# Vector instructions that stay off the port shared with GpSimd: odd row counts for the normalization, a division in PSUM, and a band mask added in PSUM

## The chip, the cores and the metric

The kernel runs on one core of a Trainium2 chip. A core has a matrix engine (TensorE, PE in the profile; its weight loads are PEld), VectorE (DVE), ScalarE (ACT), GpSimd (POOL) and SyncE (SP), which here only starts transfers. SBUF is the working memory, PSUM the memory into which TensorE writes its products, in eight banks of 128 x 512 float32. The metric is the time of one execution on the device, in microseconds (us); the median of repeated runs counts.

## The reference

One layer over x of shape (2, 256, 128, 128): batch, time, band, channel, all float32. Three parts follow each other, each with a residual: attention over time with a causal mask, attention over the bands with a band mask of width 16, and a feed-forward part with gelu.

```python
xt = _ln(x, ln_t_w, ln_t_b).transpose(0, 2, 1, 3)
x = x + _mha(xt, t_wi, t_bi, t_wo, t_bo, 4, causal).transpose(0, 2, 1, 3)
xf = _ln(x, ln_f_w, ln_f_b)
x = x + _mha(xf, f_wi, f_bi, f_wo, f_bo, 4, band)      # band: |i - j| <= 16
xn = _ln(x, ln_n_w, ln_n_b)
h = gelu(xn @ w1.T + b1)
x = x + (h @ w2.T + b2)
```

## The kernel before

The tokens are worked on in groups of 512 (four tiles of 128). There are 128 groups of each part: `OverTime`, `OverBands` and `FeedForward`. All of `OverTime` comes first, then `OverBands` and `FeedForward` in turns of eight groups. Each pass of the loop in `run` works on several groups at once, each at another stage; the engines take their instructions in the order in which the program issues them. The names below (xh, z, sp, op, rp, yp, ...) are those of the profile.

The layer norm: statistics on VectorE, the root on GpSimd (as a power of -1/2), the normalization on VectorE, one instruction for each tile of 128 elements.

```python
def root(self):
    ...
    gpsimd.tensor_scalar(self.rstd, self.mv[:, :, 1], EPS, None, ALU.add)
    gpsimd.tensor_tensor(self.rstd, self.rstd, path.k.mhalf, ALU.pow)

def normalize(self):
    path, vector = self.path, self.path.vector
    self.xh = path.work.tile([P, NT, P], F32, name="xh", bufs=2)
    for i in range(NT):
        vector.tensor_scalar(
            self.xh[:, i, :], self.src()[:, i, :], self.mv[:, i, 0:1], self.rstd[:, i : i + 1],
            ALU.subtract, ALU.mult,
        )
```

`turn` transposes xh in blocks into z and sends it through DRAM (turned); `fetch` brings it back as xnT, the input of the products.

The softmax has no maximum: exponentials of the scores sp on ScalarE, masks on GpSimd, sums of the weights as a product with ones (rp), weighted values (op). The reciprocal of rp is exp(-ln(rp)) on ScalarE (r0, r in the profile), sharpened by one Newton step on VectorE, with op multiplied in. The sign is turned back by wn, which is -wo.

```python
def divide(self):
    ...   # the exact form, for 16 of 256 groups, is cut here
    t = path.work.tile([P, NT * P], F32, name="t", bufs=2)
    vector.tensor_tensor(by_rows(t), by_tile(self.rp), by_tile(self.r0), ALU.mult)
    u = path.work.tile([P, NT * P], F32, name="u", bufs=2)
    vector.tensor_tensor(by_rows(u), by_tile(self.op), by_tile(self.r0), ALU.mult)
    self.oT = path.work.tile([P, NT * P], F32, name="oT", bufs=2)
    vector.scalar_tensor_tensor(self.oT, t, 2.0, u, ALU.subtract, ALU.mult)

def output(self):
    self.yp = path.bank([P, NT, P], "yp")       # yp = oT times wn, by tiles
    ...
def finish(self):
    self.path.vector.tensor_tensor(self.dst(), self.yp, self.dst(), ALU.add)
```

In `OverTime` a group has two halves of scores, and GpSimd masks each after its exponentials. One sum of two blocks of weights (pt) for each half is done on GpSimd (`first_mask`) and on VectorE (`last_sum`). The residual with its row is added on GpSimd (`bias`): res<-x,orow in `OverTime`, x<-x,orow in `OverBands`, res<-x,rows_sb in `FeedForward`.

In `OverBands` GpSimd masks three heads with two selections each; the fourth is multiplied by a band of ones and zeros on VectorE.

```python
def first_function(self):
    for h in range(H):
        self.path.scalar.activation(self.p[:, h].rearrange("p i q -> p (i q)"), self.sp[h], AF.Exp)

def second_mask(self):
    path = self.path
    for h in range(H - self.by_vector, H):       # by_vector = 1
        blk = self.p[:, h]
        path.vector.tensor_tensor(blk, blk, path.band.unsqueeze(1).to_broadcast([P, NT, P]), ALU.mult)
```

All PSUM tiles come from one pool of eight banks. The order of a pass:

```python
do(n + 11, "load")
do_at(n + 4, OverTime, "statistics")
...
do_at(n + 4, FeedForward, "root")
do(n, "first_half", "first_function", "first_mask")
...
do_at(n + 2, FeedForward, "normalize", "turn")
do_at(n + 3, Attention, "normalize", "turn")
do_at(n + 4, OverTime, "root")
if bands[2]:
    do(n, "second_mask")
do(n - 1, "weigh")
do(n - 1, "invert_exactly" if turn else "invert")
if bands[2] or turn:
    do(n - 2, "output", "finish")
do(n - 1, "divide")
do_at(n + 5, FeedForward, "statistics")
...
do(n + 1, "queries_keys", "take_query", "take_key")
if not bands[2] and not turn:
    do(n - 2, "output", "finish")
do(n + 1, "values", "take_values")
do(n, "last_sum")
```

Of the kernel before, what the change touches and what calls it, by code (L numbers as in the profile page):

```python
# [10 lines left out]
F32 = mybir.dt.float32  # L11
BF16 = mybir.dt.bfloat16
I32 = mybir.dt.int32
AF = mybir.ActivationFunctionType
# [5 lines left out]
P = 128  # L20
H = 4
# [404 lines left out]
def by_rows(t):  # L426

    return t.rearrange("p (t i q) -> p i t q", i=NT, q=D)


def by_tile(t):

    return t.rearrange("p (i t q) -> p i t q", i=NT, q=D)


class Group:
# [31 lines left out]
        gpsimd.tensor_tensor(self.rstd, self.rstd, path.k.mhalf, ALU.pow)  # L468

    def normalize(self):  # L470
        path, vector = self.path, self.path.vector
        self.xh = path.work.tile([P, NT, P], F32, name="xh", bufs=2)
        for i in range(NT):
            vector.tensor_scalar(
                self.xh[:, i, :], self.src()[:, i, :], self.mv[:, i, 0:1], self.rstd[:, i : i + 1],
                ALU.subtract, ALU.mult,
            )

    def turn(self):
# [19 lines left out]
    def first_function(self):  # L499
        pass  # L500
# [10 lines left out]
    def second_mask(self):  # L511
        pass
# [35 lines left out]
class Attention(Group):  # L548
# [51 lines left out]
    def divide(self):  # L600

        path, vector = self.path, self.path.vector
        if self.r0 is None:
            self.oT = path.work.tile([P, NT * P], F32, name="oT", bufs=2)
            u = path.work.tile([P, NT * P], F32, name="u", bufs=2)
            vector.tensor_tensor(by_rows(u), by_tile(self.op), by_tile(self.r), ALU.mult)
            vector.tensor_scalar(self.oT, u, -1.0, None, ALU.mult)
            return
        t = path.work.tile([P, NT * P], F32, name="t", bufs=2)
        vector.tensor_tensor(by_rows(t), by_tile(self.rp), by_tile(self.r0), ALU.mult)  # L610
        u = path.work.tile([P, NT * P], F32, name="u", bufs=2)
        vector.tensor_tensor(by_rows(u), by_tile(self.op), by_tile(self.r0), ALU.mult)
        self.oT = path.work.tile([P, NT * P], F32, name="oT", bufs=2)
        vector.scalar_tensor_tensor(self.oT, t, 2.0, u, ALU.subtract, ALU.mult)

    def output(self):
        path = self.path
# [114 lines left out]
class OverBands(Attention):  # L732
# [12 lines left out]
                path.tensor.matmul(self.sp[h][:, c], self.kT[r, c], self.qT[r, c], start=True, stop=True)  # L745

    def first_function(self):
        for h in range(H):
            self.path.scalar.activation(self.p[:, h].rearrange("p i q -> p (i q)"), self.sp[h], AF.Exp)

    def first_mask(self):
        path = self.path
        for h in range(H - self.by_vector):
            blk = self.p[:, h]
            for s in (1, -1):
# [1 line left out]
                    out=blk, in_=blk, compare_op=ALU.is_ge, fill=path.zero, base=BAND,  # L757
                    pattern=[[0, NT], [-s, P]], channel_multiplier=s,
                )

    def second_mask(self):
        path = self.path
        for h in range(H - self.by_vector, H):
            blk = self.p[:, h]
            path.vector.tensor_tensor(blk, blk, path.band.unsqueeze(1).to_broadcast([P, NT, P]), ALU.mult)

    def first_half(self):
        self.p = self.path.work.tile([P, H, NT, P], F32, name="pf", tag="p", bufs=2)
# [84 lines left out]
class BoundedPath:  # L853
    def __init__(self, ctx, tc, k):
        self.tc, self.nc, self.k = tc, tc.nc, k
        self.xpool = ctx.enter_context(tc.tile_pool(name="xpool", bufs=3))
        self.work = ctx.enter_context(tc.tile_pool(name="work", bufs=3))
        self.small = ctx.enter_context(tc.tile_pool(name="small", bufs=6))
        self.ps = ctx.enter_context(tc.tile_pool(name="ps", bufs=8, space=PSUM))
        self.tensor, self.vector = InOrder(tc, tc.nc.tensor), InOrder(tc, tc.nc.vector)  # L860
        self.scalar, self.gpsimd = InOrder(tc, tc.nc.scalar), InOrder(tc, tc.nc.gpsimd)
        self.dram = ctx.enter_context(tc.tile_pool(name="turns", bufs=3, space=DRAM))
        self.zero = 0.0
        once = ctx.enter_context(tc.tile_pool(name="once", bufs=1))

        self.band = once.tile([P, P], F32, name="band")
        tc.nc.gpsimd.memset(self.band, 1.0)
        for s in (1, -1):
            tc.nc.gpsimd.affine_select(
                out=self.band, in_=self.band, compare_op=ALU.is_ge, fill=0.0, base=BAND,  # L870
                pattern=[[-s, P]], channel_multiplier=s,
            )

# [14 lines left out]
    def quad(self, held, name, bufs):  # L888

        held[name] = self.xpool.tile([P, NT, NT, P], F32, name=name, tag=name, bufs=bufs)  # L890

    def groups(self, x, out):
        nc, k = self.nc, self.k
# [2 lines left out]
        for b in range(B):  # L896
            for f0 in range(0, FB, GA):
# [14 lines left out]
                            self.of_times(k.x1[b], i, slice(f - 1, f + 1)), held["res"][rows_of(i), :, g - 1 : g + 1]  # L912
                        )

                def part(name, g, held=held):
                    if name == "res" and name not in held:
                        self.quad(held, "res", 2)
                    return held[name][:, :, g]

                for g in range(NT):  # L920
                    yield OverTime(self, partial(part, "x", g), partial(part, "res", g), partial(load, g), partial(store, g))
        for b in range(B):
            for r0 in range(0, T, RUN):
                run = []
                for t0 in range(r0, r0 + RUN, GB):
# [17 lines left out]
                                held["res"][rows_of(i), g - 1 : g + 1].rearrange("q g t c -> q (g t) c"),  # L943
                            )

                    def part(name, g, held=held):
                        if name == "res" and name not in held:
                            self.quad(held, "res", 2)
                        return held[name][:, g]

                    run += [(g, part, load, store) for g in range(NT)]
# [5 lines left out]
    def run(self, x, out):  # L957
        groups = list(self.groups(x, out))

        def do(n, *names):  # L960
            if 0 <= n < len(groups):
                for name in names:
                    getattr(groups[n], name)()
# [11 lines left out]
        for n in range(-11, len(groups) + 2):  # L975
# [14 lines left out]
            do_at(n + 2, FeedForward, "normalize", "turn")  # L990
            do_at(n + 3, Attention, "normalize", "turn")
            do_at(n + 4, OverTime, "root")
            if bands[2]:
                do(n, "second_mask")
            do(n - 1, "weigh")
            do(n - 1, "invert_exactly" if turn else "invert")
            if bands[2] or turn:
                do(n - 2, "output", "finish")
            do(n - 1, "divide")
            do_at(n + 5, FeedForward, "statistics")  # L1000
            if not turn:
                do(n, "second_half", "second_function")
            if not bands[2]:
# [80 lines left out]
```

## Time and profile before

| what | value |
| --- | --- |
| time, median of 3 runs | 2785.62 us (2785.54 to 2787.24) |
| TensorE busy | 2730.3 us, 98% |
| VectorE busy | 2221.5 us, 80% |
| GpSimd busy | 2079.3 us, 75% |
| ScalarE busy | 1800.0 us, 65% |
| xh on VectorE | 1536 instructions, 392 ns each |
| t, u, oT on VectorE | 240 each, 667, 675 and 839 ns |
| the multiplication by the band (pf) on VectorE | 128 instructions, 935 ns each |
| res<-x,orow on GpSimd | 128 instructions, 1698 ns each |
| res<-x,rows_sb on GpSimd | 128 instructions, 1273 ns each |
| the power (rstd) on GpSimd | 384 instructions, 1149 ns each |

A line of the groups gives the source line, engine, operation, output<-inputs with shapes, the count, the busy time and the mean of one, and the idle time before them with what ended it. A line of the waits reads: engine and tile, what it waited for, then us in total, how often, and the longest. A line of the timeline gives start, duration, engine and operation; equal instructions in a row are merged, and an instruction's duration overlaps a little with the start of the next. Every operation goes through one helper, so all bear the line L848, and tiles tell them apart.

### The profile page before, as it was taken

The numbers are of one execution on the slowest core, as the hardware profiler recorded it, in microseconds if no ns is written. First come the engines' busy times: TensorE is split into PE (matmuls) and PEld (weight loads), VectorE is DVE, ScalarE is ACT, GpSimd is POOL, SyncE is SP. The second block draws the span as 40 slices with busy tenths as digits, with TensorE's granted clock in tenths as the row PEclk, the third lists the DMA queues.
The fourth block names the chain that finished last, engine by engine and source line by source line (L and its number), as shares of the span: only waits on it lengthen the run. The fifth ranks groups of instructions, "written<-read, shape, count | busy, mean of one in ns | idle before, by whom it ended". The sixth has DMA issues, their size and how long they took to land.

```text
span 2785.2 us, 103938 instructions
## 1 busy us (share of the span) xinstructions
PE 2730.3 (98%) x42534; PEld 1867.5 (67%) x42534; DVE 2221.5 (80%) x6446; ACT 1800.0 (65%) x3328; POOL 2079.3 (75%) x2569
## 2 busy tenths in 40 slices
PE   4999999999999989999999999999999999999998
PEld 3666666666666657776777777777777767767776
DVE  5888888888888898778678687687786786876874
ACT  2888888878888866646556556456466465574563
POOL 3899999999999997667676676676676666766762
PEclk9999999999999999999999999999999999999999
DMA  5555555555555554544544544535545445444333
GB/s 121 135 147 137 137 141 143 146 132 146 139 142 135 146 134 117 129 117 102 140 105 111 132 106 123 130 100 127 127 99 137 104 108 130 113 117 114 91 92 85
DMA packets 471301, 343.70 MB, mean 123 GB/s; under 512 B 43296, under 2 KB 405152, under 8 KB 470816
## 3 DMA queue, kind: packets, MB, share of 16 engines
q1 hardware_dynamic: 469568, 335.92, 47.5%
q8 instruction: 337, 5.52, 0.9%
q14 instruction: 148, 1.21, 0.2%
q10 hardware_dynamic: 1248, 1.05, 0.1%
HBM read 169.03 MB, written 167.77 MB: 121 GB/s over the span
## 4 chain that ended last, share of the span: by engine, by line
PE 93%; DVE 3%; DMA 2%; POOL 1%; issue 0%; SPq 0%; ACT 0%; DVEq 0%; POOLq 0%
PE zp L848 17%; PE hp L848 16%; PE sp L848 12%; PE op L848 10%; PE qp L848 8%; PE rp L848 8%; PE vp L848 8%; PE yp L848 7%; PE kp L848 7%; POOL pt L848 1%; DMA x<-in_x 1%; DVE xh L848 1%; DMA xnT<-turned 1%; DVE oT L848 0%; POOL rstd L848 0%; DVE stats L848 0%
## 5 line engine op out<-in xcount | busy, mean ns | idle before, releaser
L848 ACT ACTIVATE hT<-hp,b 128x512 f32<-128x512 f32 x512 | 348.7, 687 | 546.0 <-PE hp L848 536.1
L848 POOL TENSOR_SCALAR_AFFINE_SELECT pf<-pf 128x512 f32<-128x512 f32 x768 | 541.5, 720 | 173.5 <-ACT pf L848 147.1
L848 PEld LDWEIGHTS zp<-w2T_sb,hT 128*128 128x128 f32 x4096 | 476.4, 192 | 56.1 <-issue 54.0
L848 DVE TENSOR_SCALAR xh<-x,mv,rstd 128x128 f32<-128x128 f32 x1536 | 509.2, 392 | 0.4 <-POOL rstd L848 0.4
L848 PE MATMUL zp<-w2T_sb,hT 128*128 128x128 f32 x4096 | 479.8, 275 | 0.1
L848 PE MATMUL hp<-xnT,w1f 128*128 128x512 f32 x1024 | 469.2, 596 | 3.6 <-DMA xnT<-turned 3.4
L848 POOL TENSOR_TENSOR rstd<-rstd,mhalf 128x4 f32<-128x4 f32 x384 | 441.3, 1149 | 32.0
L848 ACT ACTIVATE pt<-sp 128x384 f32<-128x384 f32 x1024 | 419.5, 497 | 58.8 <-PE sp L848 58.8
L848 PE MATMUL sp<-qT,kT 32*128 32x128 f32 (+1 forms) x8192 | 389.5, 315 | 0.8 <-ACT kT L848 0.8
L848 POOL TENSOR_SCALAR_AFFINE_SELECT pt<-pt 128x512 f32<-128x512 f32 x512 | 322.7, 651 | 79.0 <-ACT pt L848 79.0
L848 PEld LDWEIGHTS sp<-qT,kT 32*128 32x128 f32 x8192 | 310.9, 185 | 79.7 <-issue 31.1
L848 POOL TENSOR_SCALAR rstd<-mv 128x4 f32<-128x4 f32 x384 | 89.2, 232 | 365.5 <-DVE mv L848 365.1
L848 DVE BATCH_NORM_STATS2 stats<-x 128x6 f32<-128x128 f32 x1536 | 329.0, 274 | 7.6 <-DMA x<-in_x 7.6
L848 ACT ACTIVATE pf<-sp 128x512 f32<-128x512 f32 x512 | 264.3, 603 | 58.8 <-PE sp L848 52.4
L848 PEld LDWEIGHTS hp<-xnT,w1f 128*128 128x128 f32 x1024 | 182.2, 190 | 178.9 <-issue 109.6
L848 PE MATMUL qp<-xnT,wf 128*32 128x512 f32 (+1 forms) x1856 | 273.1, 600 | 26.2 <-DVE xh L848 26.2
L848 PEld LDWEIGHTS yp<-wn,oT 128*32 128x32 f32 (+1 forms) x7808 | 240.8, 111 | 84.0 <-issue 63.2
L848 PEld LDWEIGHTS vp<-wf,xnT 128*32 128x32 f32 (+1 forms) x7424 | 241.1, 113 | 70.4 <-issue 60.2
L848 DVE STREAM_TRANSPOSE z<-xh 128x512 f32<-128x512 f32 x384 | 273.2, 711 | 18.9 <-DMA turned<-z 5.8
L848 PE MATMUL yp<-wn,oT 128*32 128x128 f32 (+1 forms) x7808 | 277.9, 273 | 0.3 <-DVE t L848 0.3
L848 DVE TENSOR_TENSOR res<-zp,res 128x512 f32<-128x512 f32 x128 | 87.6, 685 | 234.8 <-PE zp L848 234.7
L848 PE MATMUL vp<-wf,xnT 128*32 128x128 f32 (+1 forms) x7424 | 273.5, 273 | 0.5 <-DVE t L848 0.5
(90 smaller groups left out, 4072.8 us busy)
## 6 DMA issues: line engine op xcount, KB each, us to landing
turned<-z SPq DMA_DIRECT2D x1536, 64.0 KB, 2.2
xnT<-turned SPq DMA_DIRECT2D x384, 256.0 KB, 2.8
x<-in_x SPq DMA_DIRECT2D x128, 256.0 KB, 4.8
x<-res SPq DMA_DIRECT2D x256, 128.0 KB, 3.4
x<-x SPq DMA_DIRECT2D x128, 256.0 KB, 4.1
out<-res SPq DMA_DIRECT2D x256, 128.0 KB, 2.4
w1T_sb<-in_w1T ACTq DMA_DIRECT2D x1, 256.0 KB, 3.9
w2T_sb<-in_w2T ACTq DMA_DIRECT2D x1, 256.0 KB, 4.2
```

Of the source, the lines that this page charges most:

```text
L848: return self.tc.keep_in_program_order(emit(*args, **kwargs))
```

## The change

It is meant to keep VectorE from the accesses to SBUF that GpSimd has to wait for, and that have to wait for GpSimd.

- xh: the destination tile gets rows of 130 words, and each instruction covers 129 elements, read as one run of 129 and written as three rows of 43. The 129th element is a neighbour of the tile (the one ahead of it for the last tile, so that nothing beyond the source is read); its result falls into the padding or is overwritten by its owner.
- Division: rp is multiplied by r0 in place, in PSUM; (rp - 2) * r0 goes to u; op * u goes to oT. It is the same product in another order, and no instruction has two inputs in SBUF.
- Band: band holds 0 and -1e30 and is added to the scores of the fourth head in PSUM, ahead of its exponential. The multiplication after it is gone.
- The statistics of the feed-forward groups move ahead of the division in the order of a pass.

```diff
     def normalize(self):
         path, vector = self.path, self.path.vector
-        self.xh = path.work.tile([P, NT, P], F32, name="xh", bufs=2)
+        run, odd = P + 2, P + 1
+        xh = path.work.tile([P, NT * run], F32, name="xh", bufs=2)
+        self.xh = xh.rearrange("p (t w) -> p t w", w=run)[:, :, 0:P]
         for i in range(NT):
+            a = 1 if i == NT - 1 else 0
             vector.tensor_scalar(
-                self.xh[:, i, :], self.src()[:, i, :], self.mv[:, i, 0:1], self.rstd[:, i : i + 1],
-                ALU.subtract, ALU.mult,
+                xh[:, i * run - a : i * run - a + odd].rearrange("p (r w) -> p r w", r=3), self.src(i, a),
+                self.mv[:, i, 0:1], self.rstd[:, i : i + 1], ALU.subtract, ALU.mult,
             )
...
-        t = path.work.tile([P, NT * P], F32, name="t", bufs=2)
-        vector.tensor_tensor(by_rows(t), by_tile(self.rp), by_tile(self.r0), ALU.mult)
+        vector.tensor_tensor(self.rp, self.rp, self.r0, ALU.mult)
         u = path.work.tile([P, NT * P], F32, name="u", bufs=2)
-        vector.tensor_tensor(by_rows(u), by_tile(self.op), by_tile(self.r0), ALU.mult)
+        vector.scalar_tensor_tensor(u, self.rp, 2.0, self.r0, ALU.subtract, ALU.mult)
         self.oT = path.work.tile([P, NT * P], F32, name="oT", bufs=2)
-        vector.scalar_tensor_tensor(self.oT, t, 2.0, u, ALU.subtract, ALU.mult)
+        vector.tensor_tensor(by_rows(self.oT), by_tile(self.op), by_tile(u), ALU.mult)
...
     def first_function(self):
+        path = self.path
+        for h in range(H - self.by_vector, H):
+            sp = self.sp[h].rearrange("p (i q) -> p i q", i=NT)
+            path.vector.tensor_tensor(sp, sp, path.band.unsqueeze(1).to_broadcast([P, NT, P]), ALU.add)
         for h in range(H):
-            self.path.scalar.activation(self.p[:, h].rearrange("p i q -> p (i q)"), self.sp[h], AF.Exp)
+            path.scalar.activation(self.p[:, h].rearrange("p i q -> p (i q)"), self.sp[h], AF.Exp)
...
-    def second_mask(self):
-        path = self.path
-        for h in range(H - self.by_vector, H):
-            blk = self.p[:, h]
-            path.vector.tensor_tensor(blk, blk, path.band.unsqueeze(1).to_broadcast([P, NT, P]), ALU.mult)
...
-        tc.nc.gpsimd.memset(self.band, 1.0)
+        tc.nc.gpsimd.memset(self.band, 0.0)
...
-                out=self.band, in_=self.band, compare_op=ALU.is_ge, fill=0.0, base=BAND,
+                out=self.band, in_=self.band, compare_op=ALU.is_ge, fill=-1e30, base=BAND,
...   (the run of 129 elements out of the source, in `longer` and `part`, is cut here)
-            if bands[2]:
-                do(n, "second_mask")
+            do_at(n + 5, FeedForward, "statistics")
             do(n - 1, "weigh")
...
             do(n - 1, "divide")
-            do_at(n + 5, FeedForward, "statistics")
```

## The prediction

> **What bounds the kernel now.** I read the page first: busy time, then the waits of TensorE alone, then TensorE's busy time per stretch of 100 us, and last the timeline of single steps. The page's first part (busy us, share of the span, instructions):
>
> ```profile
> PE 2730.3 (98%) x42534; PEld 1867.5 (67%) x42534; DVE 2221.5 (80%) x6446; ACT 1800.0 (65%) x3328; POOL 2079.3 (75%) x2569
> ```
>
> TensorE leaves 2785.2 - 2730.3 = 54.9 us idle. The longest waits of TensorE (us in total, times, longest):
>
> ```profile
> PE qp L848 <- DVE xh L848: 26.2, 1, 26.2
> PE rp L848 <- DVE pt L848: 9.7, 10, 1.8
> PE hp L848 <- DMA xnT<-turned: 3.4, 5, 1.6
> ```
>
> The first is the start, before any work can reach TensorE. The third is a transfer. Only the second is a wait that VectorE or GpSimd could shorten. The table by stretches says where it lies (stretch, us, PE, PEld, DVE, ACT, POOL busy, clock, DMA share, GB/s):
>
> ```profile
> 500.00:600.00 100.00, 100.00 (x1996) 63.01 (x1992) 88.17 (x235) 80.48 (x171) 92.64 (x106) 1.00 0.54 139
> 900.00:1000.00 100.00, 95.36 (x1892) 59.66 (x1887) 91.73 (x251) 75.90 (x161) 94.63 (x109) 1.00 0.52 131
> 1000.00:1100.00 100.00, 97.05 (x1885) 65.50 (x1878) 94.91 (x235) 69.48 (x128) 83.38 (x106) 1.00 0.52 131
> ```
>
> Idle are 34.9 us in the first 100 us, 4.6 + 3.0 = 7.6 us from 900 to 1100, and 9.2 us in the last, incomplete stretch. That is 51.7 of 54.9 us; all the rest of the kernel leaves about 3 us. Since a busy TensorE need not be a fast one, I also took the distance between equal matmuls in the timeline: in attention over time a step takes 7.63 us, without change over a hundred steps, and in feed-forward 7.01 us. A cadence that exact, at a full clock, is TensorE's own. So the change can win only what lies at the start, in the passage near 1000 us and in scraps: of about 12 us a part.
>
> **What the Trainium skill says.** (1) "VectorE: DVE Perf Modes", section "What auto-detection actually checks": a one-source operation takes the two-port mode if source and destination are in SBUF and their outermost dimensions are both even, or equal. The old xh (128 to 128) meets that; the new one (129 in one row to 3 rows of 43) does not. The trace agrees on the mode of the old form: the weight scaling takes 285 ns for 128 elements and 346 for 256, so 0.48 ns an element: half a cycle of the 0.96 GHz which that page gives. (2) "SBUF — State Buffer", section "SBUF: two separate sides": VectorE in a two-port mode, or with two SBUF inputs, and GpSimd lock each other out for a whole instruction. The trace agrees: GpSimd's addition res<-x,orow takes 1698 ns in attention over time, the same shape 1273 ns as res<-x,rows_sb in feed-forward; VectorE's oT takes 690 ns undisturbed and 1770 in the passage. (3) Same page as (1), section "Why PSUM operands drop a tier": fp32 with a PSUM operand runs at one element a cycle. The trace's t, u and res, 650 to 690 ns for 512 elements, fit that; nothing here shows VectorE writing PSUM.
>
> **The change, part by part.**
>
> xh, 1536 instructions at a mean of 392 ns. Undisturbed, four take 1.08 us (band steps in the timeline), disturbed 1.4 to 2.0. At one element a cycle 129 elements cost 129/0.96 - 64/0.96 = 68 ns more than 128 at two (an estimate with the clock of that page), so four take about 1.08 + 0.27 = 1.35 us always. Mean of one: 335 + 68 = about 400 ns. VectorE's own work is not less; what is saved is GpSimd's waiting.
>
> Division: t, u, oT (667, 675, 839 ns) become rp in place, u from PSUM, oT from PSUM, 650 to 700 ns each. 240 x 0.15 = 36 us of VectorE go, none of it on TensorE's path. The bank of rp is now free after the second operation instead of the first, that of op after the third instead of the second. In attention over time the built program shows that yp waits for the bank of rp, so for u where it waited for t. This is the change's one new danger. One step of before, from 427 us:
>
> ```profile
> 427.07 0.69 DVE L848 TENSOR_TENSOR res<-yp,res 128x512 f32<-128x512 f32 x1 [0.73 <-PE yp L848]
> 427.87 1.10 DVE L848 TENSOR_TENSOR pt<-pt 128x512 f32<-128x512 f32 x1
> 428.90 0.86 DVE L848 BATCH_NORM_STATS2 stats<-x 128x6 f32<-128x128 f32 x4
> 429.96 1.40 DVE L848 TENSOR_SCALAR xh<-x,mv,rstd 128x128 f32<-128x128 f32 x4
> 431.39 0.71 DVE L848 STREAM_TRANSPOSE z<-xh 128x512 f32<-128x512 f32 x1
> 432.03 0.65 DVE L848 TENSOR_TENSOR t<-rp,r 128x512 f32<-128x512 f32 x1
> 432.60 0.67 DVE L848 TENSOR_TENSOR u<-op,r 128x512 f32<-128x512 f32 x1
> 433.57 1.06 PE L848 MATMUL yp<-wn,oT 128*32 128x128 f32 x32
> ```
>
> Before, t ends at 432.68 and yp starts at 433.57. After, from the start of xh: 1.35 + 0.03 + 0.71 (z) - 0.08 (the next operation starts that much before z is shown to end) + 0.66 + 0.03 + 0.69 = 3.39 us, and some 0.15 for the signal (what rp shows between pt's end and its own start where it does wait): 3.54. Were xh to start at 429.96 as before, that leaves 433.57 - 429.96 = 3.61, a margin of 0.07. But pt, ahead of it, waits for GpSimd's mask and shares its port (1.10 us against 0.76 in other steps). GpSimd's step loses 0.45 us of the addition and up to 0.46 of the power, so its mask and with it pt and xh come 0.2 to 0.4 us earlier. The other bound is r, which ends at 431.71: 431.74 + 1.38 + 0.15 = 433.27. Margin 0.3. I take no loss, with doubt.
>
> Band head: the multiplication pf (935 ns, two SBUF inputs) goes, and an addition in PSUM of about 680 ns comes before the last exponential. VectorE must now wait for sp at the start of the step, but ScalarE has three exponentials of 0.52 us to do first, so the fourth isn't held up. The statistics move ahead of the division. In a step with statistics and xh both, sp starts at 0, ends at 1.17; the addition runs 1.24 to 1.92, xh to 3.2, z to 3.9, statistics to 5.0, finish to 5.6, then rp, u, oT to 7.6. The next sp ends at 6.44 + 1.17 = 7.61: it just fits. What waits, the next rp matmul at 7.55, needs u, which ends near 6.9. Nothing is lost; the statistics ready earlier let GpSimd start its masks up to 0.5 us sooner.
>
> Passage. The rp matmuls from 963.21 to 1033.75 make eight steps in 70.54 us; at 7.63 they would take 61.04: 9.5 us lost. GpSimd runs there without a gap, 977.90 to 987.61:
>
> ```profile
> 977.90 1.23 POOL L848 TENSOR_SCALAR_AFFINE_SELECT pt<-pt 128x512 f32<-128x512 f32 x2
> 979.10 1.71 POOL L848 TENSOR_TENSOR res<-x,orow 128x512 f32<-128x512 f32 x1
> 980.77 1.34 POOL L848 TENSOR_TENSOR x<-x,orow 128x512 f32<-128x512 f32 x1
> 985.84 0.67 POOL L848 TENSOR_SCALAR rstd<-mv 128x4 f32<-128x4 f32 x1
> 986.59 1.04 POOL L848 TENSOR_TENSOR rstd<-rstd,mhalf 128x4 f32<-128x4 f32 x1
> 989.52 1.06 PE L848 MATMUL rp<-pt,ones 128*32 128x512 f32 x8 [1.84 <-DVE pt L848]
> ```
>
> Undisturbed, res takes 1.27 and the small addition 0.23 us: 9.71 - 0.44 - 0.44 - 0.06 = 8.77. Three steps lose 1.1 instead of 2.0: 2.8 us won. The five others (8.1 to 8.5) hold one stretched operation of 0.45 each: some 2.2 won. VectorE's step there (xh 2.04, oT 1.77) shrinks to about 8.2, below GpSimd's.
>
> The sum: 5 us in the passage, 1 in the first steps (8.36 and 8.15 us instead of 7.63), 1 in scraps of the band steps, 0.5 given back for an xh that is slower at the very start: 2785.6 - 6.5 = 2779. VectorE's busy time stays near 2220 us; GpSimd's falls by 128 x 0.43 (res) + some 100 x 0.45 (power and small addition) + 768 x 0.085 (masks) = 165 us, to about 1915.
>
> **The rivals.** First, VectorE becomes the bound in attention over time, because xh is slower, u is on yp's path, or writing PSUM costs more than reading. For it: the margin of 0.07 us without GpSimd's help; against it: that help. A lack of 0.1 us a step is 12 us: 2790; of 0.2, 2803. Second, GpSimd's relief reaches nothing, as the passage then hangs on VectorE's chain pt, xh, z, oT: 2785, the same. Third, the port was a brake in more places than the waits show, and nearly all lost time in the passage, the start and the bands comes back: 2771. Against it: the exact cadence.
>
> **Range and chances.** The most that can be won is some 15 us, the loss has a longer tail: 2771 to 2793. Faster by 2% would be 56 us, more than TensorE's whole idle time: 0.01. Slower by 2% needs 0.45 us in each of 128 steps: 0.03. Within 2%: 0.96.
>
> **What would show it.** In the changed profile: xh near 400 ns; oT, u and rp between 650 and 700; GpSimd's res<-x,orow at 1273 and the power at 1040 everywhere; steps in attention over time still 7.63; steps in the passage at most 8.8; the wait of rp for pt below 5 us. A step longer than 7.63, or a new wait of TensorE for u or sp, would prove me wrong, as would an rp in place at 900 ns.

## The result and the profile after

The changed kernel takes 2899.55 us (median of 4 runs, 2888.30 to 2905.95) where the kernel before took 2786.43 in the same comparison: a ratio of 1.0402, 95% interval 1.0364 to 1.0439. It is 4% slower. The profiled execution of it spans 2903.1 us; that of before spans 2785.2, so 117.9 us have to be found.

The page's first part (busy us, share of the span, instructions) of the changed kernel (its helper's line is L851 here; in each kernel of the experiments it has another number):

```profile
PE 2780.2 (96%) x42534; PEld 1872.9 (65%) x42534; DVE 2332.9 (80%) x6446; ACT 1806.6 (62%) x3328; POOL 1938.4 (67%) x2569
```

TensorE now idles 2903.1 - 2780.2 = 122.9 us instead of 54.9, so 68 us of the loss are open waits; in the other 50 us it shows as busy with matmuls that take longer than before. VectorE works 111 us more, though the change was to give it less. GpSimd falls by 141 us: it got much of the relief that was meant for it, and the time rose all the same. The granted clock was 0.995 in this execution and 0.999 before; e2 and e3 below lose nearly as much between them at 0.999, so the clock is not what cost the time. The chain of work that ended last, of which TensorE held 93% before:

```profile
PE 64%; DVE 24%; DMA 5%; issue 3%; SPq 1%; POOL 1%; ACT 0%; DVEq 0%; POOLq 0%
```

A quarter of the time is now set by VectorE. TensorE's longest waits (us in total, times, longest):

```profile
PE qp L851 <- DVE xh L851: 26.3, 1, 26.3
PE hp L851 <- DMA xnT<-turned: 25.9, 23, 2.2
PE yp L851 <- DVE u L851: 22.4, 56, 1.3
PE rp L851 <- DVE u L851: 10.2, 39, 0.3
PE sp L851 <- DVE u L851: 6.3, 9, 0.8
...
PE rp L851 <- DVE pt L851: 3.3, 5, 1.4
```

The first is the start, as before. The third to the fifth are waits for u, which the prediction named as what would prove it wrong. The second, feed-forward's wait for the returned transpose, was 3.4 us. The last, the one wait the change could shorten, did fall from 9.7 to 3.3 us. The table by stretches (stretch, us, PE, PEld, DVE, ACT, POOL busy, clock, DMA share, GB/s), in attention over time, the passage, and the turns of bands and feed-forward:

```profile
200.00:300.00 100.00, 99.34 (x1976) 62.99 (x1972) 83.00 (x232) 79.05 (x168) 83.73 (x105) 1.00 0.55 138
...
500.00:600.00 100.00, 95.91 (x1875) 58.74 (x1868) 91.90 (x218) 74.25 (x157) 76.47 (x98) 1.00 0.53 131
...
1000.00:1100.00 100.00, 95.71 (x1949) 60.99 (x1949) 94.76 (x232) 73.80 (x148) 89.07 (x114) 1.00 0.58 142
...
1500.00:1600.00 100.00, 96.93 (x1362) 67.56 (x1361) 81.47 (x225) 58.75 (x97) 59.88 (x85) 1.00 0.46 111
```

All but the stretch from 1000 us had TensorE at 100.00 before. In attention over time the loss comes and goes: 0.66 us in the first line, 4.09 in the second. So two stages lost, and the distance between equal matmuls (kp of one group to kp of the next) says how much each. From the fourth group to the 121st, 117 steps of attention over time take 930.9 us instead of 892.8: 38.1 lost. The eight steps of the passage that follow take 67.1 instead of 69.9: 2.8 won. One turn of eight groups over bands and eight of feed-forward takes 114.18 us in the mean instead of 109.04; the fifteen full turns lose 15 x 5.14 = 77.1. Together 112.4 of 117.9 us; nearly all the rest, 5.1, lies in the sixteenth turn.

The groups that the prediction gave a duration for (out<-in, shapes, count, busy us, mean ns of one, idle before it):

```profile
L851 DVE TENSOR_SCALAR xh<-x,mv,rstd 128x129 f32<-128x129 f32 x1536 | 662.5, 493 | 0.4 <-POOL rstd L851 0.4
...
L851 POOL TENSOR_TENSOR res<-x,orow 128x512 f32<-128x512 f32 x128 | 189.9, 1484 | 0.0
...
L851 DVE TENSOR_TENSOR oT<-op,u 128x512 f32<-128x512 f32 x240 | 166.0, 692 | 18.8 <-DVE u L851 0.9
L851 DVE SCALAR_TENSOR_TENSOR u<-rp,r 128x512 f32<-128x512 f32 x240 | 165.9, 691 | 8.2
L851 DVE TENSOR_TENSOR rp<-rp,r 128x512 f32<-128x512 f32 x240 | 164.3, 685 | 32.4 <-ACT r L851 17.6 <-PE sp L851 14.8
...
L851 DVE TENSOR_TENSOR sp<-sp,band 128x512 f32<-128x512 f32 x128 | 88.9, 695 | 128.9 <-PE sp L851 128.8
```

Three readings. The division's three operations and the addition in PSUM take what was expected, 685 to 695 ns. xh takes 493 ns in the mean, not 400, and more than the 392 of before: it is the operation that was to leave the port, and it is stretched more than ever. And the addition stands behind 128.8 us of VectorE waiting for sp.

One step of attention over time in the timeline (start us, us, engine, operation, idle before it), from one yp to the next:

```profile
498.85 1.08 PE L851 MATMUL yp<-wn,oT 128*32 128x128 f32 x32 [0.34 <-DVE u L851]
...
499.99 0.69 DVE L851 TENSOR_TENSOR res<-yp,res 128x512 f32<-128x512 f32 x1 [0.49 <-PE yp L851]
500.30 1.27 POOL L851 TENSOR_TENSOR res<-x,orow 128x512 f32<-128x512 f32 x1
500.60 1.52 DVE L851 TENSOR_TENSOR pt<-pt 128x512 f32<-128x512 f32 x1
...
502.04 0.86 DVE L851 BATCH_NORM_STATS2 stats<-x 128x6 f32<-128x128 f32 x4
...
503.10 1.73 DVE L851 TENSOR_SCALAR xh<-x,mv,rstd 128x129 f32<-128x129 f32 x4
...
503.44 1.30 POOL L851 TENSOR_SCALAR_AFFINE_SELECT pt<-pt 128x512 f32<-128x512 f32 x2 [1.88 <-ACT pt L851]
...
504.86 0.71 DVE L851 STREAM_TRANSPOSE z<-xh 128x512 f32<-128x512 f32 x1
...
505.50 0.67 DVE L851 TENSOR_TENSOR rp<-rp,r 128x512 f32<-128x512 f32 x1
...
506.20 0.69 DVE L851 SCALAR_TENSOR_TENSOR u<-rp,r 128x512 f32<-128x512 f32 x1
...
507.04 1.08 PE L851 MATMUL yp<-wn,oT 128*32 128x128 f32 x32 [0.34 <-DVE u L851]
```

This is a closed ring. yp waits for u, which gives back rp's bank; res<-yp,res waits for yp; in VectorE's order pt, the statistics, xh, z, rp and u stand behind res; and u lets the next yp go. The ring takes 507.04 - 498.85 = 8.19 us, more than TensorE's own 7.63. With the durations of the step of before shown in the prediction, the same ring is 1.14 (yp to res, taken from here) + 5.61 (from res at 427.07 to t's end at 432.68) + 0.15 (signal) = 6.90 us, so TensorE set the pace. The 1.29 us between the two are: u in the ring, which t alone was before, 0.74; xh with its gap 1.76 instead of 1.43, 0.33; pt with its gap 1.44 instead of 1.03, 0.41; a gap ahead of pt that closed, -0.19. Not every step is in it: of 120 (with the first three of the passage), 51 still take 7.6 to 7.7 us, and 63 over 7.9 (8.25 in the mean). Three were over 7.9 before. One of the 7.63 us steps of the same execution:

```profile
803.14 1.06 PE L851 MATMUL yp<-wn,oT 128*32 128x128 f32 x32
...
804.87 0.75 DVE L851 TENSOR_TENSOR pt<-pt 128x512 f32<-128x512 f32 x1
...
805.04 1.72 POOL L851 TENSOR_TENSOR res<-x,orow 128x512 f32<-128x512 f32 x1
...
806.61 1.08 DVE L851 TENSOR_SCALAR xh<-x,mv,rstd 128x129 f32<-128x129 f32 x4
```

The operations and their order on each engine are the same, u included, and yp waits for nothing. What differs is the order of two engines: here VectorE's pt starts 0.17 us before GpSimd's addition res<-x,orow, and takes 0.75 us; in the step of 8.19 us it starts 0.30 after it, and takes 1.52. So u in the ring costs nothing where pt comes first, and the ring is too long where GpSimd does. The kernel stays in one order for many steps; what tips it from one to the other is not shown.

### The profile page after: what moved, and what is told of

Read it like the earlier page. It is cut to its first block, busy times and chain, and to the rows that moved or that the text cites. A ratio compares the mean times of both kernels' runs of the same rounds, so it can differ in the third digit from the quotient of the medians.

```text
span 2903.1 us, 104133 instructions
## 1 busy us (share of the span) xinstructions
PE 2780.2 (96%) x42534; PEld 1872.9 (65%) x42534; DVE 2332.9 (80%) x6446; ACT 1806.6 (62%) x3328; POOL 1938.4 (67%) x2569
## 3 DMA queue, kind: packets, MB, share of 16 engines
q14 instruction: 151, 1.24, 0.2%
## 4 chain that ended last, share of the span: by engine, by line
PE 64%; DVE 24%; DMA 5%; issue 3%; SPq 1%; POOL 1%; ACT 0%; DVEq 0%; POOLq 0%
PE zp L851 16%; PE hp L851 15%; DVE xh L851 9%; PE sp L851 7%; PE yp L851 5%; PE op L851 5%; PE qp L851 4%; PE rp L851 4%; PE vp L851 4%; PE kp L851 4%; DVE pt L851 3%; DVE stats L851 3%; DVE u L851 2%; DVE rp L851 2%; DMA xnT<-turned 2%
## 5 line engine op out<-in xcount | busy, mean ns | idle before, releaser
L851 ACT ACTIVATE hT<-hp,b 128x512 f32<-128x512 f32 x512 | 351.4, 687 | 574.2 <-PE hp L851 565.4
L851 DVE TENSOR_SCALAR xh<-x,mv,rstd 128x129 f32<-128x129 f32 x1536 | 662.5, 493 | 0.4 <-POOL rstd L851 0.4
L851 POOL TENSOR_SCALAR_AFFINE_SELECT pf<-pf 128x512 f32<-128x512 f32 x768 | 476.0, 636 | 278.6 <-ACT pf L851 252.4
L851 PEld LDWEIGHTS zp<-w2T_sb,hT 128*128 128x128 f32 x4096 | 477.5, 192 | 56.6 <-issue 54.5
L851 PE MATMUL hp<-xnT,w1f 128*128 128x512 f32 x1024 | 471.8, 598 | 27.6 <-DMA xnT<-turned 25.9
L851 PE MATMUL zp<-w2T_sb,hT 128*128 128x128 f32 x4096 | 480.8, 276 | 0.1
L851 ACT ACTIVATE pt<-sp 128x384 f32<-128x384 f32 x1024 | 419.5, 497 | 61.5 <-PE sp L851 60.4
L851 POOL TENSOR_SCALAR_AFFINE_SELECT pt<-pt 128x512 f32<-128x512 f32 x512 | 318.3, 644 | 190.7 <-ACT pt L851 190.5
L851 PE MATMUL sp<-qT,kT 32*128 32x128 f32 (+1 forms) x8192 | 415.0, 316 | 12.8 <-DVE u L851 6.3
L851 POOL TENSOR_TENSOR rstd<-rstd,mhalf 128x4 f32<-128x4 f32 x384 | 399.2, 1040 | 32.0
L851 PEld LDWEIGHTS sp<-qT,kT 32*128 32x128 f32 x8192 | 326.4, 185 | 102.5 <-issue 31.8
L851 POOL TENSOR_SCALAR rstd<-mv 128x4 f32<-128x4 f32 x384 | 87.6, 228 | 403.5 <-DVE mv L851 403.2
L851 DVE BATCH_NORM_STATS2 stats<-x 128x6 f32<-128x128 f32 x1536 | 326.6, 273 | 7.6 <-DMA x<-in_x 7.6
L851 ACT ACTIVATE pf<-sp 128x512 f32<-128x512 f32 x512 | 268.6, 602 | 88.3 <-PE sp L851 88.0
L851 PEld LDWEIGHTS hp<-xnT,w1f 128*128 128x128 f32 x1024 | 182.5, 191 | 205.8 <-issue 118.6
L851 PEld LDWEIGHTS yp<-wn,oT 128*32 128x32 f32 (+1 forms) x7808 | 234.1, 112 | 120.4 <-PE kp L851 68.2
L851 PE MATMUL qp<-xnT,wf 128*32 128x512 f32 (+1 forms) x1856 | 271.3, 600 | 26.4 <-DVE xh L851 26.3
L851 PE MATMUL yp<-wn,oT 128*32 128x128 f32 (+1 forms) x7808 | 274.4, 274 | 22.5 <-DVE u L851 22.4
L851 DVE STREAM_TRANSPOSE z<-xh 128x512 f32<-128x512 f32 x384 | 273.2, 711 | 19.0 <-DMA turned<-z 5.9
L851 PEld LDWEIGHTS vp<-wf,xnT 128*32 128x32 f32 (+1 forms) x7424 | 240.1, 113 | 73.9 <-issue 65.6
L851 DVE TENSOR_TENSOR res<-zp,res 128x512 f32<-128x512 f32 x128 | 87.5, 684 | 237.8 <-PE zp L851 224.8
L851 PE MATMUL vp<-wf,xnT 128*32 128x128 f32 (+1 forms) x7424 | 273.5, 273 | 1.3 <-DVE u L851 1.3
```

The costliest lines, as they stand in the source:

```text
L851: return self.tc.keep_in_program_order(emit(*args, **kwargs))
```

## The experiments

The reference for all of them is the kernel before, run beside them; it took 2784.8 to 2786.4 us. "Step" is the mean of 120 distances of kp in attention over time (7.64 before), "turn" that of eight bands with eight feed-forward groups (109.04 before).

| label | what it is | us | ratio, 95% interval | step | turn |
|---|---|---|---|---|---|
| e1_xh_only | xh of 129 | 2785.7 | 1.0003, 0.9994 to 1.0012 | 7.65 | 109.1 |
| e2_division_only | division | 2807.7 | 1.0056, 1.0027 to 1.0085 | 7.97 | 108.6 |
| e3_band_only | band addition, statistics moved | 2863.5 | 1.0285, 1.0268 to 1.0302 | 7.65 | 113.7 |
| e4_stats_only | statistics moved | 2813.3 | 1.0105, 1.0088 to 1.0122 | 7.64 | 110.6 |
| e5_before_xh160 | before, xh truly one-port | 2799.8 | 1.0049, 1.0032 to 1.0066 | 7.64 | 110.2 |
| e6_after_xh160 | changed kernel, xh truly one-port | 2838.7 | 1.0177, 1.0122 to 1.0231 | 7.98 | 110.0 |
| e7_band_nostats | band addition alone | 2806.6 | 1.0077, 1.0060 to 1.0094 | 7.64 | 110.1 |
| e9_division_bands | division over bands only | 2781.8 | 0.9984, 0.9978 to 0.9991 | 7.65 | 108.8 |
| e8_op_in_place | another division, bank first | 2784.3 | 0.9992, 0.9983 to 1.0001 | 7.64 | 109.2 |
| e11_both_divisions | e8 in time, e9 over bands | 2774.9 | 0.9957, 0.9941 to 0.9974 | 7.64 | 108.7 |
| e10_op_in_place_xh160 | e8 and one-port xh | 2792.4 | 1.0021, 1.0015 to 1.0028 | 7.63 | 109.8 |
| e12_band_xh160 | e3 and one-port xh | 2796.9 | 1.0045, 1.0028 to 1.0062 | 7.64 | 110.1 |
| e13_all_bank_first | e11, e12 together | 2795.2 | 1.0033, 1.0021 to 1.0046 | 7.63 | 110.1 |

**Which part loses.** The theory was that the 129 form is neutral, as its rows melt into one, and that the division loses in attention over time and the band addition in the bands; the rival was the 129 form itself. Four kernels take the parts apart.

e1, the first part of the diff alone (t with one buffer instead of two, to make room):

```diff
-                self.xh[:, i, :], self.src()[:, i, :], self.mv[:, i, 0:1], self.rstd[:, i : i + 1],
-                ALU.subtract, ALU.mult,
+                xh[:, i * run - a : i * run - a + odd].rearrange("p (r w) -> p r w", r=3), self.src(i, a),
+                self.mv[:, i, 0:1], self.rstd[:, i : i + 1], ALU.subtract, ALU.mult,
```

> The kernel before with the 129-element xh alone (and one buffer instead of two for t, to make room). Theory A (the run of 129 is one dimension in source and destination alike, so it stays in the two-port mode, and the time is lost by the division and by the place of the band addition): four undisturbed xh still take 1.08 us, GpSimd's res<-x,orow stays at 1.70 us, time 2780 to 2800, within 0.5% of before. Theory B (the 129 form itself loses to GpSimd and that alone makes the chain slow): xh near 490 ns, 2850 to 2900.

Measured: nothing at all, 1.0003, xh 394 ns in the mean against 392 of before. Its group in e1:

```profile
L851 DVE TENSOR_SCALAR xh<-x,mv,rstd 128x129 f32<-128x129 f32 x1536 | 510.3, 394 | 0.4 <-POOL rstd L851 0.4
```

Undisturbed, one takes about 340 ns, as with 128; 196 of the 1536 take over 600 ns, up to 1334, as 196 of before do, up to 1329. In the program as built, and so in the trace, the destination is one run of 129 elements, like the source: three rows of 43 that lie end to end have become one row. The rival falls.

e2, the division alone (its part of the diff under the change, nothing else):

> The kernel before with the new division alone. Theory A: yp now waits for u, the step in attention over time goes to about 8.2 us where xh meets GpSimd, the band steps stay at 6.44: +20 to +50 us, 2805 to 2835. Theory B (129 form alone): 2780 to 2790.

Measured: 2807.7, but spread from 2783.9 to 2830.4 over 8 runs. In the profiled one 70 of 120 steps are over 7.9 us, 49 at 7.6 to 7.7, with the two orders of pt and the addition as above; the spread would come from how many steps fall into which order, but the other runs have no profile. The new wait is there without any other part of the change:

```profile
PE yp L847 <- DVE u L847: 24.0, 68, 0.7
...
PE rp L847 <- DVE pt L847: 3.5, 6, 1.4
```

The 117 steps lose 39.7 us (932.5 instead of 892.8), as in the changed kernel. But the passage wins the same 2.8 us (67.1 instead of 69.9), and each turn 0.48.

e3, the addition in PSUM with the moved statistics, and e4, the statistics moved alone:

```diff
+            do_at(n + 5, FeedForward, "statistics")
             do(n - 1, "weigh")
...
             do(n - 1, "divide")
-            do_at(n + 5, FeedForward, "statistics")
```

> The kernel before with the band added in PSUM and the statistics moved ahead of the division, nothing else. Theory A: VectorE waits for sp at the head of each band step, so that xh falls into GpSimd's masks and power; band runs go from 109 to 112-114 us, attention over time stays at 7.63: +50 to +85 us, 2835 to 2870. Theory B: 2780 to 2795.

> The kernel before with the statistics of the feed-forward groups ahead of the division, nothing else. Theory A with the band addition as the cause: within 0.3% of before, 2780 to 2792. Theory A2 (the order of the statistics, not the addition, delays the division in the band steps): +30 us or more, above 2815. Theory B: 2785.

Measured: 79 us and 29 us over the kernel before; so the place of the statistics has a cost of its own, which the first theory denied. In the bands the distance from kp to kp was 6.43 or 6.44 us in the third to sixth step; in e3 three of them become 6.85, 7.61 and 7.43, in e4 two become 6.64 and 7.16, and feed-forward behind them waits for a transpose that was sent later. Around the 7.61 us step of e3, VectorE, and below it GpSimd, in the timeline:

```profile
1625.79 0.83 DVE L846 BATCH_NORM_STATS2 stats<-x 128x6 f32<-128x128 f32 x4
...
1626.81 0.66 DVE L846 TENSOR_TENSOR x<-yp,x 128x512 f32<-128x512 f32 x1
1627.39 0.68 DVE L846 TENSOR_TENSOR t<-rp,r 128x512 f32<-128x512 f32 x1
...
1629.31 0.70 DVE L846 TENSOR_TENSOR sp<-sp,band 128x512 f32<-128x512 f32 x1
1629.92 2.63 DVE L846 TENSOR_SCALAR xh<-x,mv,rstd 128x128 f32<-128x128 f32 x4
```

```profile
1627.29 1.04 POOL L846 TENSOR_TENSOR rstd<-rstd,mhalf 128x4 f32<-128x4 f32 x1
1629.83 3.92 POOL L846 TENSOR_SCALAR_AFFINE_SELECT pf<-pf 128x512 f32<-128x512 f32 x6 [1.50 <-ACT pf L846]
```

The scores end at 1629.28 (1626.93 + 2.35, in the lines below). ScalarE's exponential waits for them (1.49 us), and GpSimd's masks for the exponential (1.50 us); VectorE, late itself, reaches the addition just as they end. So xh and the masks now start together, at 1629.92 and 1629.83. Four xh take 2.63 us instead of 1.08, one for each mask (3.92 / 6 = 0.65 us a mask, 2.63 / 4 = 0.66 an xh). That delays x<-yp,x and t of the next step, which stand behind statistics now, and they are what gives TensorE its banks for the scores. TensorE's weight loads and products for the scores in the same step of e3:

```profile
1626.92 0.30 PEld L846 LDWEIGHTS sp<-qT,kT 32*128 32x128 f32 x4 [0.20 <-ACT kT L846]
1626.93 2.35 PE L846 MATMUL sp<-qT,kT 32*128 32x128 f32 x32
...
1627.52 0.29 PEld L846 LDWEIGHTS sp<-qT,kT 32*128 32x128 f32 x2 [0.30 <-DVE x L846]
...
1628.12 0.96 PEld L846 LDWEIGHTS sp<-qT,kT 32*128 32x128 f32 x26 [0.30 <-DVE t L846]
```

The scores, shown as busy for 2.35 us instead of 1.17, stop for x and for t; the late scores hold up the exponential and the masks, so that these meet xh. A second ring, and it shows why TensorE can lose time while it is shown as busy.

**Is it the port, or VectorE's order?** For that xh has to leave the two-port mode in truth. e5, e6 and later runs write five rows of 32 out of one run of 160; the rows lie 34 apart and can't be merged. 32 columns more are computed for each tile than are needed. To make room, e5 and e12 have one buffer instead of two for t and for u, e10 and e13 for t alone.

```diff
+        Q, G = D + 2, NT + 1
+        xh = path.work.tile([P, NT * G, Q], F32, name="xh", bufs=2)
...
+                xh[:, i * G - a : i * G - a + G, 0:D], self.src(i, a * D),
```

> The kernel before, with an xh whose rows cannot be merged: 160 elements read in one run, written as 5 rows of 32 that lie 34 apart (32 columns of the neighbour tile are computed too and overwritten, or lie ahead of the last tile and are computed again; t and u get one buffer instead of two to make room). Theory A (the 3 rows of 43 lie end to end and became one run of 129 on both sides, so the two-port mode was never left; this form does leave it): one xh is about 100 ns longer when undisturbed (337 to about 440), never above 500 even beside GpSimd, and GpSimd's res<-x,orow falls from 1700 to 1273 us in attention over time; GpSimd's busy time falls by some 60 us. The step of 7.63 us leaves little room, time 2780 to 2800. Theory B (the mode has nothing to do with it; 128 or 160 elements meet GpSimd in the same way): xh still shows 650 to 800 ns beside GpSimd, res<-x,orow stays near 1700.

Measured in e5: xh 426 ns in the mean and never above 445, beside GpSimd as without it; so this form doesn't wait for the port. The price is its length: four take 1.57 instead of 1.08 us, and the kernel 14 us more, which lie in the turns (15 x 1.16 us). One buffer less for t cost nothing in e1; what the one less for u has of the 14 us is not separated. One thing was expected wrongly: GpSimd's addition of attention over time is as long as ever.

```profile
L851 DVE TENSOR_SCALAR xh<-x,mv,rstd 128x160 f32<-128x160 f32 x1536 | 592.2, 426 | 14.5 <-POOL rstd L851 0.4
...
L851 POOL TENSOR_TENSOR res<-x,orow 128x512 f32<-128x512 f32 x128 | 219.6, 1715 | 0.0
```

Its partner at the port isn't xh.

> The changed kernel with the same unmergeable xh of 5 rows of 32 out of 160. Theory A (the loss of the changed kernel comes from its division and its band addition, and the failed xh only takes away the cure): the lock between xh and GpSimd goes, so the slow regime of attention over time (8.20 us a step, where four xh take 1.73 us) shrinks, and in the bands xh no longer shows 784 ns; yet four undisturbed xh now take about 1.45 instead of 1.08 us, so a part stays: 2820 to 2870. Theory B (the loss is only VectorE's order, whatever the lock does): xh gets longer for nothing, 2900 or more. Theory C (the lock is all of it): 2775 to 2800.

> Band addition and moved statistics (2863.5 us with an xh of 128), with the division of before and the unmergeable xh of 5 rows of 32 out of 160 (t and u with one buffer). Theory A (in the band steps the addition and the statistics move xh into the time of GpSimd's rstd, and xh in the two-port mode waits there for the port, 784 ns and more): no xh over 500 ns, GpSimd undisturbed, and most of the 79 us gone: 2795 to 2815, where this xh alone made 2800. Theory B (the order itself, VectorE waiting for sp at the head of the step, is the cost): xh is longer still, 2870 or more.

e6 against the changed kernel, and e12 against e3, differ in xh's form (e12 also in one buffer less of t and u). e6: the turns fall from 114.18 to 110.01 us, the time from 2899.6 to 2838.7, while the time steps stay long, 7.98 (7.96 in the changed kernel). e12: 2863.5 becomes 2796.9, no more than the 2799.8 of e5, which has the same xh and no addition. A step of e12 to be laid beside that of e3:

```profile
1609.90 0.70 DVE L849 TENSOR_TENSOR sp<-sp,band 128x512 f32<-128x512 f32 x1
1610.51 1.60 DVE L849 TENSOR_SCALAR xh<-x,mv,rstd 128x160 f32<-128x160 f32 x4
```

The order is that of e3, xh stands directly behind the addition and beside GpSimd's masks (from 1610.43), and takes 1.60 us; the step is 6.44 us. So in the bands it is the port: with an xh off the port the addition and the early statistics cost nothing, and with a two-port xh 79 us, because they push it into GpSimd's time.

e6 also shows the time steps with an xh of constant length, 1.57 us for four. Counted from yp to yp, 23 of its steps take 7.63 us, with pt first and 0.74 us long in the mean; 96 take 8.10 in the mean, nearly all with the addition first and pt 1.52 long. With xh off the port, the order of pt and the addition alone separates the two.

e7, the addition with the statistics left at the end, asks whether the two only hurt together:

> The kernel before, with the band head's addition in PSUM in place of its multiplication, and the statistics of feed-forward left where they were, at the end of the step. Band addition with moved statistics cost 79 us, moved statistics alone 29. Theory A (the addition at the head of the step, which holds VectorE until sp is there, is a cost of its own): 79 - 29 = 50 us, about 2835, the steps with xh 6.8 to 7.2 us. Theory B (the two together overflow the step; the addition alone fits): 2780 to 2790. Theory C (statistics early were needed by the addition): above 2863.

Measured: 2806.6, between the theories: the addition alone costs some 20 us, the statistics alone 29, both 79. Both push xh the same way: behind 1100 us, 62 xh took over 500 ns before, 177 do in e4, 241 in e7, 443 in e3, and none in e12.

**What makes the ring in attention over time.** The division was next tried where it had shown a gain:

```diff
+        if self.which == OverBands.which:
+            ...   # rp in place, u, oT from op and u, as in the change
+            return
```

> The kernel before, with the new division in attention over bands only; attention over time keeps t, u, oT as before. Theory A (the loss of the division alone, 20 us, is all in the time steps, while in the bands it won about 0.48 us in each of 16 runs): time steps 7.64 us, band runs 108.5 instead of 109.0, so 8 us less: 2774 to 2780, the fastest so far. Theory B (the gain in the bands came with the shifted schedule of the time steps): 2784 to 2788.

Measured: steps 7.65 again, turns 108.8, in all 2781.8, 0.16% faster. A real gain, but half of what was expected: a turn is 0.24 us shorter in the mean, not 0.48, and the passage is as long as before (70.4 against 69.9 us). Then a division that keeps off two SBUF sources too, but gives rp's bank back after its first operation, as before:

```diff
-        vector.tensor_tensor(by_rows(t), by_tile(self.rp), by_tile(self.r0), ALU.mult)
-        ...
-        vector.tensor_tensor(by_rows(u), by_tile(self.op), by_tile(self.r0), ALU.mult)
-        vector.scalar_tensor_tensor(self.oT, t, 2.0, u, ALU.subtract, ALU.mult)
+        vector.tensor_tensor(t, self.rp, self.r0, ALU.mult)
+        vector.tensor_tensor(self.op, self.op, self.r0, ALU.mult)
+        vector.scalar_tensor_tensor(self.oT, t, 2.0, self.op, ALU.subtract, ALU.mult)
```

> The kernel before, with a division that also keeps off two SBUF sources but gives rp's bank back after its first operation: t from rp into SBUF, op times r in place in PSUM, oT from t and op (all three over contiguous columns; the output's matmuls pick their 32 columns). Theory A (the 8.20 us step of the new division is a closed loop: u gives the bank to yp, yp's end lets res<-yp,res start, and res stands ahead of pt, statistics, xh, z and rp in VectorE's order, so an operation more before yp lengthens the loop): with t as the first operation the loop is 0.7 us shorter and TensorE sets the step again, 7.63 to 7.70 us, and res<-x,orow falls to 1273; 2772 to 2785. Theory B (the step grows because oT leaves the port free and GpSimd's addition then meets VectorE's pt, which takes 1.5 instead of 1.1 us): the same happens here, steps of 7.9 to 8.2 us, 2805 to 2825.

Measured in e8: the steps are 7.64, 118 of 120 at 7.63, and none of TensorE's longer waits is one of yp for VectorE. The ring no longer sets the pace, with every operation of the division off the port. The time, 2784.3, is at the long end of what was expected, and one detail was wrong: res<-x,orow stays at 1706 ns. The timeline of e8 shows why:

```profile
504.33 0.72 DVE L849 TENSOR_TENSOR pt<-pt 128x512 f32<-128x512 f32 x1
...
504.47 1.71 POOL L849 TENSOR_TENSOR res<-x,orow 128x512 f32<-128x512 f32 x1
```

Here VectorE's pt, with two SBUF sources, starts 0.14 us before GpSimd's addition and takes 0.72, and the addition waits (1.71). In the changed kernel the addition starts 0.30 us before pt and takes 1.27, and pt waits (1.52). GpSimd pays 0.44 us in the one order, VectorE 0.80 in the other; which of them pays is decided by who comes first. The Trainium skill, "SBUF — State Buffer", section "SBUF: two separate sides", says just that: whichever starts first has the pair for its whole instruction. Both traces agree. In e8 pt comes first in every step. That its ring would bear the other order too rests on a sum: 8.19 - 0.74 = 7.45 us (an estimate from the step above).

**Both together, and the change as meant.**

> The division of the run before (rp's bank free after the first operation) in attention over time, and the change's division in attention over bands, where it won 5 us. Theory A: both gains add: 2768 to 2780, the fastest of all. Theory B (the time steps run in the long regime with any division off the port): 2800 to 2820.

> The kernel before with the division that frees rp's bank first, and the unmergeable xh of 5 rows of 32 (one t buffer): the aim of the change, both operations off the port, without its band addition. Theory A: GpSimd is disturbed only by VectorE's pt; the longer xh costs what it cost alone (14 us over the kernel before), so 2785 to 2800. Theory B (with nothing left to make GpSimd wait, xh's extra length is hidden in the passage): 2770 to 2785.

> The change as it was meant, all of it: xh really off the port (5 rows of 32 out of 160, one t buffer), the division off the port with rp's bank free first in attention over time and the change's own division over bands, the band addition and the moved statistics. Theory A (the port is the cause of all losses in the bands, the bank of those in time): time steps 7.63, runs 109.5 to 110, 2780 to 2800, no better than the two divisions alone (2774.9), since the longer xh costs some 8 to 14 us and the addition gains TensorE nothing. Theory B (the aim was right and only spoiled): below 2770. Theory C (the order of the band step costs by itself): above 2830.

e11, the division of e8 in attention over time and that of the change over bands, takes 2774.9 us, 0.43% faster than the kernel before and the fastest of all; TensorE's waits in it, after the one at the start:

```profile
PE rp L863 <- DVE pt L863: 4.3, 4, 1.4
PE bp L357 <- DMA cols_sb<-in_cols: 3.6, 1, 3.6
PE hp L863 <- DMA xnT<-turned: 2.4, 3, 1.5
```

The wait of rp for pt is down from 9.7 to 4.3 us, the eight steps of the passage take 65.9 us instead of 69.9, and a turn 0.3 less than before. e10 shows that a one-port xh beside the same kind of division as in e8 costs 8 us rather than helps. e13, all three parts of the change with xh really off the port and rp's bank free first, takes 2795.2: both rings are gone (steps 7.63, turns 110.1), so the loss of the changed kernel is gone with them. It is 20 us behind e11, 1.33 us a turn; the xh of 160 alone cost 0.58 (e10 against e8) to 1.16 (e5). So the addition gains nothing that shows.

## Why the prediction was wrong

**The bound** was read rightly: TensorE at 7.63 us a step, little to win. The passage's gain was right too in mechanism: the wait of rp for pt fell from 9.7 to 3.3 us, and the passage's eight steps are 2.8 us shorter where 5 were predicted (4.0 in e11).

**The step that failed first** is "the new one (129 in one row to 3 rows of 43) does not" meet the condition of the two-port mode. The Trainium skill's condition ("VectorE: DVE Perf Modes", section "What auto-detection actually checks") was applied to the view in the source text, not to the pattern in the built program: there it is 129 on both sides, odd but equal, and equality is enough by that section. e1 agrees: 394 against 392 ns, and as many stretched ones as before. So "four take about 1.35 always" was 1.08 when alone and 1.73 or more beside GpSimd. The estimate of the one-port cost itself was fair: worked out as in the prediction, with that page's clock, 160/0.96 - 64/0.96 = 100 ns more for 160 elements, and e5's undisturbed ones show up to 440 ns where those of 128 show 340.

**The second step** is "I take no loss, with doubt" for yp. From the start of xh to yp the prediction counted 3.54 us; the step shown took 507.04 - 503.10 = 3.94, and 0.38 of the difference is xh at 1.73 instead of 1.35. That is the first error coming back. But the step had one of its own: that GpSimd's relief would let pt and xh come 0.2 to 0.4 us earlier. In the step of 7.63 us shown above that came true: xh starts 806.61 - 804.26 = 2.35 us after res, where it was 429.96 - 427.07 = 2.89 before. In the longer ones GpSimd reached its addition before VectorE's pt instead of after it, and pt went from 1.10 to 1.52 us: there the help had the wrong sign. The prediction asked only how soon GpSimd is done, and not which of the two engines comes first. And the margin was taken on one stretch of a ring instead of around it: u's 0.74 us are added to every round, as yp's end is what starts VectorE's chain. Had xh taken 1.35 us, the ring would still be 8.19 - 0.38 = 7.81 us, over 7.63 (an estimate from this step), and e6, with xh off the port at 1.57, indeed stays at 7.98 in the mean. Nor was xh or oT what stretched GpSimd's addition, as the prediction had it: it takes 1715 ns in e5 with xh off the port 1706 in e8 with oT off it and 1716 in e10 with both off it; in their timelines it starts while pt runs. The first rival, VectorE as the bound in attention over time through u on yp's path, is what happened, with some 0.3 us a step where it allowed 0.1 to 0.2.

**The third and costliest step** is "it just fits ... Nothing is lost" for the band head. Its sum for the heavy step put the addition at 1.24 to 1.92 and xh at 3.2, so 1.3 us for four. The addition's length was right (695 ns), the place was right, but four xh took 2.63, as they meet GpSimd's masks there. "The statistics ready earlier let GpSimd start its masks up to 0.5 us sooner" had no worth. Most of the 77 us of the turns are this step's (e3 alone has turns of 113.7 us): TensorE's sp waits for the banks that x and t (u in the changed kernel) give back. With the xh that the prediction had assumed, e12 shows the step would have been right: 6.44 us.

**Not predicted:** that xh alone would be without effect, and that a kernel with little idle time in TensorE has so little slack in VectorE's order behind it. The range reached 7 us above the time of before; the two rings cost 115.

## What to carry to other kernels

Check a view that is meant to break a rule of the access pattern in the built program, as rows that lie end to end become one row, and look at the maxima of the operation's duration beside the other engine, not at the mean alone. When an in-order engine both frees a bank and waits for what fills it, add up the whole ring and compare it with the bound's cadence: one more operation before the bank is freed counts once in every round. Do the sum for both orders of two engines that share a port, since the same program can run in either. Freeing the bank with the first operation kept TensorE's pace (e8) and, with the change's division over bands, won 0.43% (e11). An operation that is moved is worth what it meets in its new place.

## What the runs showed of the hardware

Of two operations at the shared port the later one pays: pt 0.72 and GpSimd's addition 1.71 us with pt first, 1.52 and 1.27 with the addition first. Four short two-port operations beside a row of GpSimd's masks do not wait once but about once each, 0.66 us an xh at 0.65 us a mask: 2.63 us instead of 1.08. VectorE writing a product in place into PSUM (685 ns) costs the same as reading PSUM and writing SBUF (691), which the kernel before could not show.
